# A two-layer graph network on one core: layer 2 gathers raw rows first, normalisation is stored behind it, and the table work is spread differently

## The chip, the cores and the metric

One of the eight cores of a Trainium2 chip runs the kernel. The metric is the device time of one execution in microseconds (us), less being better. The profile is of one such execution. TensorE appears in it as PE (weight loads as PEld), VectorE as DVE, ScalarE as ACT, GpSimd as POOL; SP issues most of the DMAs, in order, ACT and POOL issue some.

## The reference, cut to what matters

There are N = 6250 nodes with 128 features and E = 106250 edges, sorted by target node. Two attention layers ("conv") run over the edges, with a normalisation over all nodes between them:

```python
rel_t_enc = jnp.cos((last_update[src] - t)[:, None] * time_w[None, :] + time_b)
edge_attr = jnp.concatenate([rel_t_enc, msg], axis=-1)          # 32 + 64 columns
h = _transformer_conv(x, edge_attr, src, dst, Wq1, ..., bs1)     # 2 heads
mu = h.mean(axis=0)
var = ((h - mu) ** 2).mean(axis=0)
h = (h - mu) / jnp.sqrt(var + 1e-05) * bn_g + bn_b               # per feature, over all nodes
h = jax.nn.relu(h)
return _transformer_conv(h, edge_attr, src, dst, Wq2, ..., bs2)
# around it: layernorm(x + that), row by row
# _transformer_conv: q = h Wq + bq, k = h Wk + bk, v = h Wv + bv, e = edge_attr We, all in 2 heads;
#   alpha = q[dst] . (k[src] + e) / 8; softmax over the edges of a target;
#   out = segment_sum(a * (v[src] + e)) + h Ws + bs
```

Layer 2 can't begin with normalised rows before the last node of layer 1 is done, because the mean and the variance are over all nodes.

## The kernel before

**Chunks and rounds.** The edges are cut into 107 chunks (NC) of 1024 edges, each with at most 64 target nodes. `conv(c, extra)` runs a software pipeline of rounds k = -4 to 109, written out by hand: each engine executes its instructions in the order in which the rounds emit them. In round k chunk k+4 is fetched and gathered, chunk k+1 is transposed, chunk k is scored, chunk k-1 is summed and chunk k-2 is finished.

- `fetch(k)` (L720 to L738): SP issues the DMAs of the edge attributes into `ff`, of the table rows into `ftab`, and in layer 2 of the stored time encoding `fz`, of the transposed attributes (into `fxT`) and of the residual rows `fr`. `ff` and `ftab` have six buffers.
- `gather(k)` (L743): eight indirect DMAs of 128 source rows each, issued by POOL; from `xv_d` in layer 1, from `h_d` in layer 2.
- `turn_in` (L792, L798): TensorE transposes the gathered rows and, in layer 1, the attributes; ACT copies them out of PSUM (L793, L799). The PSUM tiles of these, of the turned weights (L832) and of the extra work come from one pool of four banks.
- `score`, `lowest`, `weigh` (L809, L810, L815, L817, L822): the scores, their row minimum `flow` on DVE, and the exponential on ACT.
- `gather_sums` (L839), `divide` (L844 to L847, giving `fa`), `finish_turn` (L853, L854, and the copy `fat`, L856), `finish` (L863 on): the weighted sums. In layer 1, `finish` adds the residual table into `fres` (L869) and stores 64 columns of `hT` by a DMA (L870).

**The time encoding** exists in layer 1 alone. `encode(j)` is nine DVE instructions (L760 to L768); `sine()` is one ACT instruction (L774) that writes `fzs`, after a load of the sine's table (ACT_TABLE_LOAD; the exponential loads its own again). In the next round `place()` copies `fzs` into `ff` (DVE, L779) and stores it to `enc_d` (SP, L780). Up to chunk 26 (SINGLE = 24, and three more) one chunk is encoded per sine and per round; after that two chunks share a sine, every second round. `fzs` has two buffers.

**Tables and other extra work.** Layer c's queries are folded with the key weights into table rows per node, in 13 blocks of 512 nodes (`tables`): four or five matmuls (L627), each followed by an ACT instruction (L631, L629) or a DVE one (L633) into `fo`, then a store to `tab_d` (L637, issued by ACT). They are yielded step by step by `rest()` and pulled by the rounds, `pull(extra, 1)` per round, six steps more at the first round of layer 1. Layer 2's blocks have five steps, the last a residual (`residual`, L1030 to L1033). Blocks 0 and 1 of layer 2 are made before its pipeline begins, through a single PSUM bank.

**Between the layers** come, in this order: a sum of `hT` (half on DVE, half on ACT, L983), the squares (L988), the square root and four small steps, then 13 blocks of scaling with Relu on ACT (L1003), transposing (L1006), copying to `fhr` (L1008, four buffers) and storing to `h_d` (L1011, L1014). Layer 2's first gather waits for all of `h_d`.

Of the kernel before, what the change touches and what calls it, by code (L numbers as in the profile page):

```python
# [7 lines left out]
F32 = mybir.dt.float32  # L8
# [612 lines left out]

def tables(nc, pl, c, fT, b0, work, bank):

    o = work.tile([P, GE, H, 3 - c], F32, name="fo", tag="fo")
    for i, (a, b) in enumerate(pl.mats[c]):
        pg = bank()
        nc.tensor.matmul(pg, a, fT, start=True, stop=True)  # L627
        if i == 2 * H:
            nc.scalar.activation(o[:, :, :, 2], pg[:, :, None].to_broadcast([P, GE, H]), AF.Identity, bias=b)  # L629
        elif i < H:  # L630
            nc.scalar.activation(o[:, :, i, 0], pg, AF.Identity, bias=b)  # L631
        else:
            nc.vector.scalar_tensor_tensor(  # L633
                o[:, :, i - H, 1].rearrange("p (b n) -> p b n", n=P), pg.rearrange("p (b n) -> p b n", n=P), b,
                pl.code[:, None, :].to_broadcast([P, GE // P, P]), op0=OP.add, op1=OP.add)
        if i == len(pl.mats[c]) - 1:
            nc.scalar.dma_start(pl.tab_d[c][:, b0 * GE:(b0 + 1) * GE], o)  # L637
        yield
# [22 lines left out]
def ordered(ctx: ExitStack, tc: tile.TileContext, pl, x, dst, edge_attr_64, conv2, bn_g, bn_b, out):  # L661
# [9 lines left out]
    const = ctx.enter_context(tc.tile_pool(name="fconst", bufs=1))  # L671
    dram = ctx.enter_context(tc.tile_pool(name="fdram", bufs=1, space=bass.MemoryType.DRAM))
    h_d = dram.tile([N, D], F32, name="h_d")
    res_d = dram.tile([NP, D], F32, name="res_d")

    enc_d = dram.tile([NC, P, T * TD], F32, name="enc_d")
# [14 lines left out]

    SINGLE = 24

    def conv(c, extra):


        cs = ExitStack()
# [42 lines left out]
        def gather(k):  # L740
            f = ch[k].f
            for t in range(T):
                nc.gpsimd.indirect_dma_start(  # L743
                    out=f[:, t, (1 if c else 0):1 + D], out_offset=None, in_=h_d if c else pl.xv_d,
                    in_offset=bass.IndirectOffsetOnAxis(ap=pl.srcs[:, t, k:k + 1], axis=0))

        shape = [P, T, TD]
# [22 lines left out]
        def sine():  # L770
            arg, *of = args
            args.clear()
            z = work.tile([P, 2, T, TD], F32, name="fzs")
            nc.scalar.activation(z[:, :len(of)], arg[:, :len(of)], AF.Sin, bias=qpi)  # L774
            turned.extend((k, z[:, i]) for i, k in enumerate(of))

# [6 lines left out]
        def turn_in(k, u):  # L783

            s = ch[k]
            if u == 0:
                s.ft = work.tile([P, CE], F32, name="fft")
                if c == 0:
                    s.et = work.tile([EC, CE], F32, name="fet")
            px = p_tr.tile([P, GE], F32, name="fpx", tag="tr")  # L790
            for t in range(4):
                nc.tensor.transpose(px[:, t * P:(t + 1) * P], s.f[:, u * 4 + t, 1:1 + D], ident)  # L792
            nc.scalar.copy(s.ft[:, u * GE:(u + 1) * GE], px)  # L793
            if c:
                return
            pe = p_tr.tile([P, GE], F32, name="fpe", tag="tr")
            for t in range(4):
                nc.tensor.transpose(pe[:EC, t * P:(t + 1) * P], s.f[:, u * 4 + t, 1 + D:], ident)  # L798
            nc.scalar.copy(s.et[:, u * GE:(u + 1) * GE], pe[:EC])  # L799
            if u:  # L800
                nc.sync.dma_start(et_d[k], s.et)
# [39 lines left out]
        def divide(k):  # L841
            s = ch[k]
            inv = small.tile([P, 1], F32, name="finv")
            nc.vector.tensor_scalar(inv, s.pa[:, D + ED:], 1e-30, None, op0=OP.max)  # L844
            nc.vector.reciprocal(inv, inv)
            s.a = small.tile([P, D + EW], F32, name="fa")
            nc.vector.tensor_scalar(s.a, s.pa, inv, None, op0=OP.mult)  # L847

        def finish_turn(k):
            s = ch[k]  # L850
# [60 lines left out]
        with cs, tc.manual_schedule():  # L911
            for k in range(-AHEAD, NC + 3):
# [3 lines left out]
                if on(k + AHEAD):  # L916
                    fetch(k + AHEAD)
                    gather(k + AHEAD)
                if k == -AHEAD and c == 0:
                    pull(extra, 6)  # L920
                if on(k):
                    score(k, 0)
                if on(k - 1):
# [16 lines left out]
                for j in (k + 2,) if k < SINGLE else (k + 2, k + 3) if k == SINGLE else (k + 3,):  # L940
                    if c == 0 and on(j):
                        encode(j)
                        if j < SINGLE + 3:
                            sine()
                pull(extra, 1)
                if len(args) == 3 or args and k == NC - 4:
                    sine()
                if on(k - 2):
                    finish(k - 2)
                if c and on(k):  # L950
                    nc.vector.tensor_copy(ch[k].f[:, :, 1 + D:1 + D + TD], ch[k].z)
                for _ in range(min(len(done), 2 if k > NC - 12 else 1)):
                    store(*done.pop(0))
                if on(k - 1):
                    gather_sums(k - 1)
            for _ in extra:
                pass
            for rows in done:
# [5 lines left out]
    with tc.tile_pool(name="fpw", bufs=2) as pw:  # L964
        with tc.tile_pool(name="ftp", bufs=3, space=bass.MemoryType.PSUM) as mp, tc.manual_schedule():
            turn_features(nc, pl, mp, N)
        def rest():
            for b0 in range(1, NT):
                yield from tables(nc, pl, 0, xT[:, b0 * GE:(b0 + 1) * GE], b0, pw, lambda: pl.bank())
                if b0 == 2:  # L970
                    yield from load_others(nc, pl, const, conv2, bn_g, bn_b)
            yield from matrices(nc, pl, 1, const, lambda: pl.bank()[:, :P])

        conv(0, rest())
    nc.gpsimd.memset(hT[:, N:], 0.0)


    with tc.tile_pool(name="fbn1", bufs=1) as one, tc.tile_pool(name="fbnw", bufs=2) as pw:
        neg = one.tile([P, 2], F32, name="fmu")
        half = N // 2  # L980
        scr = pl.xT
        nc.vector.tensor_reduce(neg[:, 0:1], hT[:, :half], AX.X, OP.add)
        nc.scalar.activation(scr[:, half:N], hT[:, half:N], AF.Copy, accum_out=neg[:, 1:])  # L983
        mu = one.tile([P, 1], F32, name="fmu1")
        nc.vector.tensor_add(mu, neg[:, 0:1], neg[:, 1:])
        nc.vector.tensor_scalar(mu, mu, -1.0 / N, None, op0=OP.mult)
        var = one.tile([P, 1], F32, name="fbvar")
        nc.scalar.activation(scr[:, :N], hT[:, :N], AF.Square, bias=mu, accum_out=var)  # L988
        nc.vector.tensor_scalar(var, var, 1.0 / N, EPS, op0=OP.mult, op1=OP.add)
        nc.scalar.activation(var, var, AF.Sqrt)  # L990
        scale = one.tile([P, 1], F32, name="fscale")
        nc.vector.reciprocal(scale, var)
        nc.vector.tensor_mul(scale, scale, pl.bng)
        shift = one.tile([P, 1], F32, name="fshift")
        nc.vector.tensor_mul(shift, scale, mu)
        nc.vector.tensor_add(shift, shift, pl.bnb)
        NB = -(-N // P)
        with tc.tile_pool(name="fbnh", bufs=4) as hp, \
                tc.tile_pool(name="fbnp", bufs=2, space=bass.MemoryType.PSUM) as pps:
            for b0 in range(0, NB, 4):  # L1000
                n = min(4, NB - b0)
                cs_ = slice(b0 * P, b0 * P + GE)
                nc.scalar.activation(hT[:, cs_], hT[:, cs_], AF.Relu, bias=shift, scale=scale)  # L1003
                pt = pps.tile([P, 4, P], F32, name="fpt")
                for i in range(n):
                    nc.tensor.transpose(pt[:, i], hT[:, (b0 + i) * P:(b0 + i + 1) * P], ident)  # L1006
                hr = hp.tile([P, 4, P], F32, name="fhr")
                nc.vector.tensor_copy(hr[:, :n], pt[:, :n])  # L1008
                full = min(n, (N - b0 * P) // P)
                if full:  # L1010
                    nc.sync.dma_start(h_d[b0 * P:(b0 + full) * P, :].rearrange("(b p) d -> p b d", p=P), hr[:, :full])  # L1011
                if full < n:
                    left = N - (b0 + full) * P
                    nc.sync.dma_start(h_d[(b0 + full) * P:N, :], hr[:left, full])  # L1014

        def residual(b0):

# [21 lines left out]
            next(res, None)  # L1039
            yield  # L1040

        with tc.tile_pool(name="fpp2", bufs=1, space=bass.MemoryType.PSUM) as pp:
            pl.bank = lambda: pp.tile([P, GE], F32, name="fpg")
            for b0 in range(2):
                for _ in block(b0):
                    pass

        def rest():
            for b0 in range(2, NT):
                yield from block(b0)  # L1050

        conv(1, rest())
    nc.sync.dma_start(out[N - NN:N, :], tail_d[NN:2 * NN, :])


@with_exitstack
def tile_gnn_resnorm(ctx: ExitStack, tc: tile.TileContext, x, src, dst, edge_attr_64, edge_weight, node_vec,
# [13 lines left out]
    with tc.tile_pool(name="plan", bufs=1) as pl, tc.tile_pool(name="planw", bufs=2) as mw, \  # L1071
# [5 lines left out]
                                                  ap=[[step, r1 - r0], [1, P]]))  # L1077
        NP = got.NP = -(-(N + NN) // GE) * GE
        got.hT = keep.tile([P, NP], F32, name="fhT")
        got.rest = keep.tile([P, 1 + D], F32, name="fxrest")  # L1080
        got.raw, got.web, got.ws, got.mats = {}, {}, {}, ([], [])

# [22 lines left out]
        nc.vector.tensor_scalar(ident, jpp, 0.0, None, op0=OP.is_equal)  # L1105
        nxt = pl.tile([P, NC], F32, name="nxt")
        nc.vector.tensor_scalar(nxt, jpp[:, :NC], 1.0, None, op0=OP.is_equal)
        ones = pl.tile([P, P], F32, name="pones")
        nc.vector.memset(ones, 1.0)
        ends = pl.tile([1, 2, NC + 1], F32, name="ends")  # L1110
        nc.vector.memset(ends[:, 0, NC:], float(N))
# [154 lines left out]
```

## Time and profile before

| | us |
|---|---|
| median of 11 runs (2327.93 to 2334.68) | 2332.75 |
| the profiled execution, its own time | 2332.44 |
| its span | 2330.3 |
| first and last gather issued, layer 1 | 38.2, 1145.5 |
| first and last gather issued, layer 2 | 1220.5, 2290.4 |
| row minimum L815 of chunk 2, 26 and 106, layer 1 | 90.05, 349.60, 1175.46 |
| busy: PE, POOL, DVE, ACT | 2226.6, 1639.5, 1224.5, 1222.1 |

2.1 us of the time lie outside the span. A round can be read as the distance between two row minima L815, since each chunk has one. A matmul's end is modelled, so that a full PE row says that PE had work queued, not that it was at its peak.

### The profile page before, as it was taken

Reading aid. Unit: us, or ns where it says so; the run is one execution under the profiler, and the core shown is the slowest. Engines: PE = TensorE matmul, PEld = TensorE weight load, DVE = VectorE, ACT = ScalarE, POOL = GpSimd, SP = SyncE. Lnnn points to the kernel's source line nnn. Section 1 sums busy time; section 2 is a strip of 40 time slices with the busy share of each in tenths; the row PEclk is TensorE's granted clock in tenths of the full one; section 3 lists DMA queues with packets and bytes.
Section 4 is the critical chain, followed back from the end, with each engine's and each line's share of the span. In section 5 each row is a group of like instructions: output and inputs, shape, how many; then the busy total and the mean of one; then the engine's idle time right before and its main releaser. Section 6 shows DMA issues by size and latency. Waiting matters only on the chain.

```text
span 2330.3 us, 39250 instructions
## 1 busy us (share of the span) xinstructions
PE 2226.6 (96%) x11637; PEld 1715.4 (74%) x11637; DVE 1224.5 (53%) x3735; ACT 1222.1 (52%) x1950; POOL 1639.5 (70%) x1733
## 2 busy tenths in 40 slices
PE   6899999999999999999958999999999999999997
PEld 4778878788787888878844777777777777776765
DVE  5667677677676766666633443433343333333333
ACT  3667776666655555555543444444444444343444
POOL 3777777777777777777507777777777777777772
PEclk8999999999999999999977999999999999999999
DMA  8666666666665665665529667776667666656561
GB/s 256 173 154 185 178 191 189 181 180 179 180 181 159 163 160 156 166 160 157 141 71 247 176 186 194 191 189 189 183 180 188 166 164 165 166 155 161 156 155 36
DMA packets 428354, 396.58 MB, mean 170 GB/s; under 512 B 282064, under 2 KB 371940, under 8 KB 424804
## 3 DMA queue, kind: packets, MB, share of 16 engines
q1 hardware_dynamic: 354406, 238.66, 37.0%
q0 software_dynamic: 55168, 114.12, 20.4%
q10 hardware_dynamic: 18558, 41.20, 5.0%
q8 instruction: 95, 1.56, 0.3%
q14 instruction: 127, 1.04, 0.1%
HBM read 279.72 MB, written 110.59 MB: 167 GB/s over the span
## 4 chain that ended last, share of the span: by engine, by line
PE 40%; POOL 4%; DMA 4%; issue 2%; DVE 1%; ACT 1%; POOLq 0%; ACTq 0%; DVEq 0%
PE fpa L839 13%; PE fps L809 7%; PE fps L810 7%; POOL ff L743 4%; PE fpx L792 3%; PE fppt L832 3%; DMA ff<-h_d,fsrcs 3%; PE fpg L627 2%; PE fpo L875 2%; PE fpo L876 1%; PE fpg L1030 1%; PE fpo L853 0%; PE fpo L854 0%; DVE flow L815 0%; DMA h_d<-fhr 0%
## 5 line engine op out<-in xcount | busy, mean ns | idle before, releaser
L743 POOL DMA_INDIRECT ff<-xv_d,fsrcs x856 | 824.7, 963 | 311.0 <-issue 212.8
L743 POOL DMA_INDIRECT ff<-h_d,fsrcs x856 | 810.2, 946 | 290.5 <-issue 258.8
L839 PE MATMUL fpa<-ff,fpt 128*128 128x225 f32 x3424 | 700.0, 357 | 0.0
L839 PEld LDWEIGHTS fpa<-ff,fpt 128*128 128x128 f32 x3424 | 633.4, 190 | 11.1 <-issue 0.5
L833 ACT COPY fpt<-fppt 128x512 f32<-128x512 f32 x428 | 229.4, 588 | 464.8 <-PE fppt L832 463.5
L809 PE MATMUL fps<-fft,ftab 128*128 128x512 f32 x856 | 445.2, 602 | 5.2 <-ACT fs L822 5.2
L793 ACT COPY fft<-fpx 128x512 f32<-128x512 f32 x428 | 249.0, 582 | 378.8 <-PE fpx L792 375.4
L856 DVE COPY fat<-fpo 128x256 f32<-128x256 f32 x214 | 90.9, 425 | 577.9 <-PE fpo L854 573.9
L822 ACT ACTIVATE fs<-fps,fm 128x1024 f32<-128x1024 f32 x214 | 238.6, 1115 | 88.0 <-DVE fm L817 87.0
L832 PEld LDWEIGHTS fppt<-fident,fs 128*128 128x128 f32 x1712 | 200.1, 140 | 105.9 <-issue 105.6
L815 DVE TENSOR_REDUCE flow<-fps 128x1 f32<-128x1024 f32 x214 | 260.1, 1215 | 9.8 <-PE fps L810 9.8
L792 PE MATMUL fpx<-fident,ff 128*128 128x128 f32 x1712 | 246.6, 274 | 15.0 <-DMA ff<-h_d,fsrcs 14.5
L832 PE MATMUL fppt<-fident,fs 128*128 128x128 f32 x1712 | 222.2, 272 | 0.0
L810 PE MATMUL fps<-fet,ftab 112*128 112x512 f32 x428 | 219.2, 593 | 0.0
L810 PE MATMUL fps<-fxT,ftab 112*128 112x512 f32 x428 | 219.1, 593 | 0.0
L792 PEld LDWEIGHTS fpx<-fident,ff 128*128 128x128 f32 x1712 | 198.6, 141 | 24.8 <-DMA ff<-h_d,fsrcs 20.8
L809 PEld LDWEIGHTS fps<-fft,ftab 128*128 128x128 f32 x856 | 167.7, 225 | 8.0 <-ACT fs L822 6.0
L810 PEld LDWEIGHTS fps<-fet,ftab 112*128 112x128 f32 x428 | 107.3, 251 | 76.0 <-issue 59.8
L810 PEld LDWEIGHTS fps<-fxT,ftab 112*128 112x128 f32 x428 | 84.3, 197 | 99.7 <-issue 99.5
L767 DVE SCALAR_TENSOR_TENSOR farg<-fturns,farg 128x256 f32<-128x256 f32 x321 | 136.6, 426 | 11.0
L844 DVE TENSOR_SCALAR finv<-fpa 128x1 f32<-128x1 f32 x214 | 32.8, 153 | 206.3 <-issue 94.9
L798 PE MATMUL fpe<-fident,ff 128*112 128x128 f32 x856 | 130.7, 276 | 7.7 <-DVE ff L779 5.1
(198 smaller groups left out, 2272.3 us busy)
## 6 DMA issues: line engine op xcount, KB each, us to landing
ff<-in_edge_attr SPq DMA_DIRECT2D x214, 256.0 KB
et_d<-fet SPq DMA_DIRECT2D x107, 448.0 KB
fxT<-et_d SPq DMA_DIRECT2D x107, 448.0 KB
ftab<-tab_d SPq DMA_DIRECT2D x107, 192.0 KB
tab_d<-fo ACTq DMA_DIRECT2D x13, 1536.0 KB
ff<-xv_d,fsrcs POOLq DMA_INDIRECT x856
enc_d<-fzs SPq DMA_DIRECT2D x107, 128.0 KB
ff<-h_d,fsrcs POOLq DMA_INDIRECT x856
```

Source lines behind the costliest of these rows:

```text
L743: nc.gpsimd.indirect_dma_start(out=f[:, t, (1 if c else 0):1 + D], out_offset=None, in_=h_d if c else pl.xv_d, in_offset=bass.IndirectOffs ...
L767: nc.vector.scalar_tensor_tensor(arg, turn, -part, arg, op0=OP.mult, op1=OP.add)
L792: nc.tensor.transpose(px[:, t * P:(t + 1) * P], s.f[:, u * 4 + t, 1:1 + D], ident)
L793: nc.scalar.copy(s.ft[:, u * GE:(u + 1) * GE], px)
L798: nc.tensor.transpose(pe[:EC, t * P:(t + 1) * P], s.f[:, u * 4 + t, 1 + D:], ident)
L809: nc.tensor.matmul(s.ps[:, w], s.tab[:, :, 0], s.ft[:, w], start=True, stop=False)
L810: nc.tensor.matmul(s.ps[:, w], s.tab[:EC, :, 1], s.et[:, w], start=False, stop=True)
L815: nc.vector.tensor_reduce(low, s.ps, AX.X, OP.min)
L822: nc.scalar.activation(s.s, s.ps, AF.Exp, bias=s.bias, scale=-1.0)
L832: nc.tensor.transpose(pp[:, t * P:(t + 1) * P], s.s[:, at:at + P], ident)
L833: nc.scalar.copy(s.pt[:, u * GE:(u + 1) * GE], pp)
L839: nc.tensor.matmul(s.pa, s.pt[:, t * P:(t + 1) * P], s.f[:, t, 1:1 + D + EW], start=t == 0, stop=t == T - 1)
```

## The change

Layer 1's rounds now also transpose finished blocks of `hT`, take their moments (`bn_stats`) and store them raw to `h_d`. The first three chunks of layer 2 gather from `h_d` and are normalised after the gather: by ACT on the way out of PSUM, and in place on DVE (`normalise`, three instructions on 128x1024). Meanwhile all rows are normalised, transposed and stored to `hn_d`, from which the other chunks gather. The sums and squares over the whole of `hT` are replaced by one `bn_aggr` over the blocks' moments, and scale and shift are spread over partitions by two DVE steps, two matmuls and a copy. `turned_rows` makes four transposes and one DVE copy of a block, `put_rows` its DMA. One block of tables instead of two stands ahead of layer 2, with three PSUM banks; no step is pulled before round 0, then two per round up to round 3 and after round 80, and each block is followed by two empty steps. `fo` and `fzs` have one buffer, and the row tile `fhr` is in a pool of two.

```diff
 def tables(nc, pl, c, fT, b0, work, bank):
-    o = work.tile([P, GE, H, 3 - c], F32, name="fo", tag="fo")
+    o = work.tile([P, GE, H, 3 - c], F32, name="fo", tag="fo", bufs=1)
...
+    RAW = 3
-    def conv(c, extra):
+    def conv(c, extra, first_blocks=None):
...
-                    out=f[:, t, (1 if c else 0):1 + D], out_offset=None, in_=h_d if c else pl.xv_d,
+                    out=f[:, t, (1 if c else 0):1 + D], out_offset=None, in_=(h_d if k < RAW else hn_d) if c else pl.xv_d,
...
-            z = work.tile([P, 2, T, TD], F32, name="fzs")
+            z = work.tile([P, 2, T, TD], F32, name="fzs", bufs=1)
...
-            nc.scalar.copy(s.ft[:, u * GE:(u + 1) * GE], px)
+            if c and k < RAW:
+                nc.scalar.activation(s.ft[:, u * GE:(u + 1) * GE], px, AF.Relu, bias=pl.shift, scale=pl.scale)
+            else:
+                nc.scalar.copy(s.ft[:, u * GE:(u + 1) * GE], px)
...
+        def normalise(k):
+            rows = ch[k].f[:, :, 1:1 + D]
+            for i, op in enumerate((OP.mult, OP.add)):
+                nc.vector.tensor_tensor(rows, rows, pl.spread[:, None, i].to_broadcast([P, T, D]), op)
+            nc.vector.tensor_scalar(rows, rows, 0.0, None, op0=OP.max)
...
-                if k == -AHEAD and c == 0:
-                    pull(extra, 6)
+                if k == -AHEAD and c:
+                    first_blocks()
...
-                pull(extra, 1)
+                if k >= 0:
+                    at_round[0] = k
+                    pull(extra, 2 if k < 4 or k > 80 else 1)
...
                 if c and on(k):
+                    if k < RAW:
+                        normalise(k)
...
+        def pass_rows(b0):
+            r0 = b0 * GE
+            n = min(GE, N - r0)
+            rows = turned_rows(b0)
+            nc.vector.bn_stats(stats[:, b0], hT[:, r0:r0 + n])
+            yield
+            put_rows(h_d, b0, rows)
+            yield
...
         def rest():
+            others = load_others(nc, pl, const, conv2, bn_g, bn_b)
             for b0 in range(1, NT):
                 yield from tables(nc, pl, 0, xT[:, b0 * GE:(b0 + 1) * GE], b0, pw, lambda: pl.bank())
-                if b0 == 2:
-                    yield from load_others(nc, pl, const, conv2, bn_g, bn_b)
+                for _ in range(2):
+                    next(others, None)
+                    yield
             yield from matrices(nc, pl, 1, const, lambda: pl.bank()[:, :P])
+            for b0 in range(-(-N // GE)):
+                while at_round[0] < 3 + max(k for k in range(NC) if first(k)[0] < (b0 + 1) * GE):
+                    yield
+                yield from pass_rows(b0)
         conv(0, rest())
...
...
+        moments = const.tile([P, 2], F32, name="fmom")
+        nc.vector.bn_aggr(moments, stats)
...
+        def relu(b0):
+            r = slice(b0 * GE, (b0 + 1) * GE)
+            nc.scalar.activation(hT[:, r], hT[:, r], AF.Relu, bias=shift, scale=scale)
+        def first_blocks():
+            for b0 in range(1, NT):
+                relu(b0)
+            for b0 in range(-(-N // GE)):
+                put_rows(hn_d, b0, turned_rows(b0))
-        with tc.tile_pool(name="fpp2", bufs=1, space=bass.MemoryType.PSUM) as pp:
-            for b0 in range(2):
-                for _ in block(b0):
-                    pass
+        with tc.tile_pool(name="fpp2", bufs=3, space=bass.MemoryType.PSUM) as pp, tc.manual_schedule():
+            relu(0)
+            for _ in block(0):
+                pass
...
         def rest():
-            for b0 in range(2, NT):
+            for b0 in range(1, NT):
                 yield from block(b0)
+                yield
+                yield
-        conv(1, rest())
+        conv(1, rest(), first_blocks)
```

More of the change, by code (lines that the diff above doesn't have):

```diff
@@ L673, in ordered @@
     h_d = dram.tile([N, D], F32, name="h_d")
+    hn_d = dram.tile([N, D], F32, name="hn_d")
+    at_round = [0]
+    stats = const.tile([P, -(-N // GE), 6], F32, name="fstats")
     res_d = dram.tile([NP, D], F32, name="res_d")
@@ L955, in conv @@
                     gather_sums(k - 1)
+            at_round[0] = 2 * NC
             for _ in extra:
@@ L966, in ordered, with turned_rows @@
             turn_features(nc, pl, mp, N)
+        def pass_rows(b0):
[6 more added lines that the diff above has]
+            yield
+        def turned_rows(b0):
+            r0 = b0 * GE
+            n = -(-min(GE, N - r0) // P)
+            pt = pl.bank().rearrange("p (b d) -> p b d", d=P)
+            for i in range(n):
+                nc.tensor.transpose(pt[:, i], hT[:, r0 + i * P:r0 + (i + 1) * P], ident)
+            rows = pw.tile([P, GE // P, P], F32, name="fhr")
+            nc.vector.tensor_copy(rows[:, :n], pt[:, :n])
+            return rows
@@ L967, in rest, with put_rows @@
+        def put_rows(to, b0, rows):
+            r0 = b0 * GE
+            n = min(GE, N - r0)
+            full = n // P
+            if full:
+                nc.sync.dma_start(to[r0:r0 + full * P, :].rearrange("(b p) d -> p b d", p=P), rows[:, :full])
+            if n > full * P:
+                nc.sync.dma_start(to[r0 + full * P:N, :], rows[:n - full * P, full])
         def rest():
+            others = load_others(nc, pl, const, conv2, bn_g, bn_b)
             for b0 in range(1, NT):
                 yield from tables(nc, pl, 0, xT[:, b0 * GE:(b0 + 1) * GE], b0, pw, lambda: pl.bank())
-                if b0 == 2:
-                    yield from load_others(nc, pl, const, conv2, bn_g, bn_b)
+                for _ in range(2):
+                    next(others, None)
+                    yield
@@ L972, in rest @@
             yield from matrices(nc, pl, 1, const, lambda: pl.bank()[:, :P])
+            for b0 in range(-(-N // GE)):
+                while at_round[0] < 3 + max(k for k in range(NC) if first(k)[0] < (b0 + 1) * GE):
+                    yield
+                yield from pass_rows(b0)
         conv(0, rest())
[L975 to L992, printed above, removed]
-        nc.vector.tensor_mul(scale, scale, pl.bng)
[L994 to L1014, printed above, removed]
@@ new lines, in ordered @@
+        moments = const.tile([P, 2], F32, name="fmom")
+        nc.vector.bn_aggr(moments, stats)
+        std = const.tile([P, 1], F32, name="fstd")
+        nc.vector.tensor_scalar(std, moments[:, 1:], EPS, None, op0=OP.add)
+        nc.scalar.activation(std, std, AF.Sqrt)
+        scale = pl.scale = const.tile([P, 1], F32, name="fscale")
+        nc.vector.reciprocal(scale, std)
+        nc.vector.tensor_mul(scale, scale, pl.bng)
+        shift = pl.shift = const.tile([P, 1], F32, name="fshift")
@@ L1016, in residual @@
+        nc.vector.tensor_mul(shift, scale, moments[:, 0:1])
+        nc.vector.tensor_sub(shift, pl.bnb, shift)
         def residual(b0):
@@ L1040, in block @@
             yield
-        with tc.tile_pool(name="fpp2", bufs=1, space=bass.MemoryType.PSUM) as pp:
-            pl.bank = lambda: pp.tile([P, GE], F32, name="fpg")
-            for b0 in range(2):
-                for _ in block(b0):
-                    pass
+        def relu(b0):
[7 more added lines that the diff above has]
+        with tc.tile_pool(name="fpp2", bufs=3, space=bass.MemoryType.PSUM) as pp, tc.manual_schedule():
+            pl.bank = lambda: pp.tile([P, GE], F32, name="fpg")
+            relu(0)
+            for _ in block(0):
+                pass
+            diag = const.tile([P, 2, P], F32, name="fdiag")
+            spread = pl.spread = const.tile([P, 2, P], F32, name="fspread")
+            pb = pp.tile([P, 2, P], F32, name="fpb", bufs=1)
+            for i, col in enumerate((scale, shift)):
+                nc.vector.tensor_scalar(diag[:, i], ident, col, None, op0=OP.mult)
+                nc.tensor.matmul(pb[:, i], pl.ones, diag[:, i], start=True, stop=True)
+            nc.vector.tensor_copy(spread, pb)
         def rest():
-            for b0 in range(2, NT):
+            for b0 in range(1, NT):
                 yield from block(b0)
-        conv(1, rest())
+                yield
+                yield
+        conv(1, rest(), first_blocks)
     nc.sync.dma_start(out[N - NN:N, :], tail_d[NN:2 * NN, :])
@@ L1079, in tile_gnn_resnorm @@
         got.hT = keep.tile([P, NP], F32, name="fhT")
+        nc.gpsimd.memset(got.hT[:, N:], 0.0)
         got.rest = keep.tile([P, 1 + D], F32, name="fxrest")
@@ L1107, in tile_gnn_resnorm @@
         nc.vector.tensor_scalar(nxt, jpp[:, :NC], 1.0, None, op0=OP.is_equal)
-        ones = pl.tile([P, P], F32, name="pones")
+        ones = got.ones = keep.tile([P, P], F32, name="pones")
         nc.vector.memset(ones, 1.0)
```

## The prediction

> **What bounds the kernel now.** I read the page's slices first, then the two layers' gathers, then one round of layer 1 and the border between the layers in the timeline.
>
> ```profile
> PE   6899999999999999999958999999999999999997
> POOL 3777777777777777777507777777777777777772
> PEclk8999999999999999999977999999999999999999
> ```
>
> PE is full but for the start and one hole in the middle; only there does its clock drop. The hole is the border between the layers.
>
> ```profile
> L743 POOL DMA_INDIRECT ff<-xv_d,fsrcs x856: 938/944/1194, 38.2 to 1145.5; - x172
> L743 POOL DMA_INDIRECT ff<-h_d,fsrcs x856: 940/944/1399, 1220.5 to 2290.4; - x172
> ```
>
> These rows answer for the gathers' tile. Layer 2's 856 gathers take 1070 us, 1.25 us each, 10.0 per chunk of eight: POOL never waits there. Its row minima L815 stand 10.14 us apart while table steps run and 9.28 after them, so PE first falls behind and then catches POOL up: layer 2 ends when its gathers end, wherever they began. Layer 1 differs: 107 chunks at 10.0 would be 1070 us, and its gathers take 1107. There PE sets the pace: rounds of 9.83 us without a table step, 10.69 with one (0.86 us of PE each). Here is one such round of the first 27, in which each round has its own sine:
>
> ```profile
> 197.23 1.22 DVE L815 TENSOR_REDUCE flow<-fps 128x1 f32<-128x1024 f32 x1
> 201.81 1.28 ACT L774 ACT_TABLE_LOAD   x1
> 202.39 0.54 DVE L869 TENSOR_TENSOR fres<-fpo,ftab 64x64 f32<-64x64 f32 x2
> 202.95 0.34 SPq L731 DMA_DIRECT2D ftab<-tab_d  x1
> 203.10 0.51 ACT L774 ACTIVATE fzs<-farg,qpi 128x256 f32<-128x256 f32 x1
> 203.41 0.36 SPq L780 DMA_DIRECT2D enc_d<-fzs  x1
> 203.64 0.29 DVE L779 COPY ff<-fzs 128x256 f32<-128x256 f32 x1
> 204.36 0.45 DVE L847 TENSOR_SCALAR fa<-fpa,finv 128x225 f32<-128x225 f32 x1
> 207.16 0.27 PE L853 MATMUL fpo<-fident,fa 128*128 128x128 f32 x1
> 207.92 1.21 DVE L815 TENSOR_REDUCE flow<-fps 128x1 f32<-128x1024 f32 x1
> ```
>
> The reader should see the order in SP's queue. The store of `fzs` (L780) stands behind the table fetch (L731), which waits for `fres` (ends 202.93). So the store at 203.41 is not that of the sine at 203.10 but of the sine one round earlier: counting both from the start, store 13 leaves at 203.41 and sine 14 starts at 203.10. With two buffers that harms nobody, and DVE's `fa` is ready 2.35 us before PE asks for it at 207.16.
>
> Last, the border:
>
> ```profile
> 1190.27 2.81 ACT L983 ACTIVATE fxT<-fhT 128x3125 f32<-128x3125 f32 x1 [9.32 <-DMA fhT<-fres]
> 1201.63 9.28 ACT L1003 ACTIVATE fhT<-fhT,fshift,fscale 128x512 f32<-128x512 f32 x13 [0.87 <-DVE fshift L996]
> 1220.55 0.95 POOL L743 DMA_INDIRECT ff<-h_d,fsrcs  x1 [29.91 <-issue]
> 1228.16 0.36 ACTq L637 DMA_DIRECT2D tab_d<-fo  x1
> 1250.52 0.94 POOL L743 DMA_INDIRECT ff<-h_d,fsrcs  x1 [0.30 <-issue]
> ```
>
> Layer 1's last `hT` store lands at 1190.2; the first gather starts 30.4 us later, chunk 3's first (1250.52) 60.3 us later.
>
> **The border, changed: -18.7 us.** Let L be the landing of the last `hT` store. Raw rows of the earlier blocks are stored by then; the last block needs one transpose, one copy, one small DMA (3.4 us from issue to use, from L1014 at 1215.85 to SP's next step at 1219.2) and POOL's start 1.3 us after that, so chunk 0's gather starts near L+6 and POOL has chunks 0 to 2 out at L+36. Chunk 3 needs all of `hn_d`. Its chain: transpose, copy, `bn_stats`, `bn_aggr` (no row shows either; by the DVE rows of 128x106, 0.24, and 128x512, 0.69, they cost 0.2 to 0.7 each; I take 0.3, the small form being nearer), square root and five small steps of 0.2: L+2.6. ACT then has eight scalings of 0.71 (9.28/13), two L631 of 1.16 and an issue of 0.4 before the table store: L+11.8. SP's table fetch of chunk 0 waits for its landing (1228.16 to 1232.26: 4.1), and with three more issues behind it the first `hn_d` store leaves at L+17.9. All 14 stores stand in SP's queue there, ahead of chunk 1's fetch. `fhr` now has two buffers: copy 0.69 plus store 2.5 to 2.7 (issue 1206.33, its buffer's next copy 1208.82) make 3.4 us per two blocks; six such turns, a small last store of 2.3 and POOL's start give L+41.6. So chunk 3 comes 60.3 - 41.6 = 18.7 earlier. Bounds: a gain of 24 if the stores keep up and only the 30 us of gathers count; 9 if each store takes the 4.1 us that one took before. PE's own start is earlier too (its first transposes stand behind the 13 blocks, at about L+32, against 1251.07, L+60.9), chunk 1's fetch leaves at L+39 against L+46.8, and the three `normalise` steps (by L815's 1.22 for 1024 elements, 3.7 us per chunk) lie on a DVE that is under 40% busy there; without that cover they would cost 11. Relu instead of a copy out of PSUM is 0.71 against 0.58, six times, on an idle ACT.
>
> **Layer 2: 0.** Five table steps in seven rounds give PE 9.28 + 0.86 x 5/7 = 9.9 per round, under POOL's 10.0. POOL sets the pace and the end moves with its start.
>
> **`fzs` with one buffer: +52.** Sine n must now wait for store n-1, and the sine's table load with it, since in the changed program's instruction order the wait stands on the load. In rounds 2 to 25, where the table fetch is held by `fres`, a turn closes: row minimum to end of `fres` 5.70 (197.23 to 202.93); to the store's issue 0.48; the store's packets end 2.1 to 2.9 after issue in these rounds, median 2.35, and I take 2.45 with its signal; load 1.28 and sine 0.51, with 0.1 between; then from the sine's end to the next row minimum 2.14, which one round shows where the sine came last:
>
> ```profile
> 128.77 0.51 ACT L774 ACTIVATE fzs<-farg,qpi 128x256 f32<-128x256 f32 x1
> 130.62 0.30 PE L853 MATMUL fpo<-fident,fa 128*128 128x128 f32 x1 [1.84 <-DVE fa L847]
> 131.41 1.21 DVE L815 TENSOR_REDUCE flow<-fps 128x1 f32<-128x1024 f32 x1
> ```
>
> Together 12.6 us per round, against PE's 9.83 or 10.69. What is queued behind the waiting load on ACT: the sine, a table step, the two copies of turned weights (PE's sums and PSUM banks wait for them); behind the sine on DVE: L779, `divide`, and so PE's L853. The 24 rounds from minimum 2 to 26 took 349.60 - 90.05 = 259.6. Now 24 x 12.6 = 302.4, six rounds with a DVE table step before `fres` at 0.97 more (the store leaves 7.15 instead of 6.18 after the minimum), and one round that encodes twice, 3.3: 311.5. After round 26 two chunks share a sine every second round, so that about ten microseconds lie between store and sine, and nothing waits. The cheap end for this cost is zero (then these rounds take 254, the pace of PE alone); the dear end is 13.4 per round, with stores of 2.9 and half-clocked matmuls on the way: +71.
>
> At this place a page speaks. In the rows, the load takes 1.28 us and the sine starts 0.01 after it. The Trainium skill, "ScalarE: Activation LUTs", section "What ACT_TABLE_LOAD costs", adds a drain of some 1.38 us to each switch. By it, as an estimate, the 24 rounds would cost another 33 us; I go by the rows.
>
> **The rest of layer 1: +11.6, and 0.75 at its end.** Rounds 0 to 2: four table steps now fall into rounds 0 and 1, where two ACT ones (1.16 each) stand before the copies for PE's first sums, and 0.86 of PE each: +2.9. Rounds 26 to 106 took 1175.46 - 349.60 = 825.9, some 7 of it late waits for gathers. Now: 80 x 9.83 = 786.4; the 38 table steps left at 0.86, 32.7; layer 2's matrices as before, 5; eleven blocks of `pass_rows` at four transposes (0.12 each), 5.5; and 5 for their 1.3 us on DVE (copy 0.69, `bn_stats` 0.6) in rounds where a sine stands just before: 834.6, +8.7. PE is ahead of nothing it could make up: POOL needs 10.15 per chunk there. Block 11's copy and moments delay the last `fres` by 0.75. Hidden, all at nothing: SP's 14 raw stores (0.36 each, in a queue with room), the earlier memset (0.44 on an idle POOL), and `fo` with one buffer, whose store (5.6 to 7.7 us) has a whole round before the next write.
>
> **The sum** against the profiled execution: 2332.44 + 2.9 + 52.0 + 8.7 + 0.75 - 18.7 = 2378.1. That execution lies 0.3 us under the median; I say 2378. About 0.2% (5 us) is what a measurement of this kernel can tell from no change.
>
> **Rivals.**
> 1. *The sine's wait does not bind* (its store gets out before the table fetch, or lands in time). Then -5.5 takes the place of +52: 2320.6, faster. For it: with two buffers the trace has no such wait. Against it: store 13 after sine 14. It turns on one number: the turn has to fall below 10.6 us, which the store would reach only by leaving 2 us earlier than the end of `fres` lets it.
> 2. *The clock falls as well.* In the round above, 1.84 us of idle PE was followed by 3.4 us at half clock (131.06 to 134.47), with four L792 in 0.87 instead of 0.60. Now each such round idles 2 to 3 us. One slow stretch costs PE some 1.7 and still fits (9.83 + 0.86 + 1.7 = 12.4); two per round make 14.1, 36 more: 2414. By the Trainium skill, "TensorE: Matmul & The Clock Gate", Part 1, the clock falls after an idle window of 3.4 us; by that estimate it would not fall here at all, while the row shows it after 1.84.
> 3. *The border gives nothing back* (`hn_d` late, or chunk 3 held by a later DMA): 2397.
>
> **How the numbers follow.** Forecast 0.76; rival 1 0.11; rival 2 0.06; rival 3 0.07. The forecast's own range is 2356 to 2398 (turn of 11.9 to 13.4, border 9 to 24). Rival 3 lies inside it; rivals 1 and 2 are left out: 2350 to 2399. Faster 0.11, same 0.02, slower 0.87.
>
> **What would show it.** Right: row minima of layer 1's chunks 3 to 26 about 12.6 apart, ACT's idle time before the sine's table load ended by the `enc_d` store, PE at 8 tenths in slices 3 to 7, the last `hT` landing near 1255, chunk 3's gather 42 us after it, layer 2 at 10.0 per chunk. Wrong: minima at 10.4 there, or a first gather of `hn_d` 60 us after the landing.

## The result, and the profile after

The changed kernel takes 2386.07 us (median of 8 runs, 2384.05 to 2388.25), the kernel before in the same session 2332.3: a ratio of 1.0232 (95% interval 1.0223 to 1.0241), slower by 54 us. The forecast was 2378, in a range of 2350 to 2399. The profiled execution has a span of 2384.9 us, 54.6 more than before.

The page's slices first:

```profile
PE   5888888999999999999996999999999999999996
POOL 3766555777777777677724777777777777777772
PEclk7999999999999999999997999999999999999998
```

PE is at 8 tenths in the third to seventh slice, where it was at 9: in them lie most of the rounds in which each chunk has a sine of its own. The hole in the middle is still there and narrower. The gathers' rows, from the view of their line, now L748 (duration least/median/most, first and last start):

```profile
L748 POOL DMA_INDIRECT ff<-xv_d,fsrcs x856: 938/944/1197, 39.0 to 1212.0; - x172
L748 POOL DMA_INDIRECT ff<-h_d,fsrcs x24: 940/944/1007, 1264.3 to 1293.1; - x24
L748 POOL DMA_INDIRECT ff<-hn_d,fsrcs x832: 940/944/1482, 1302.7 to 2344.4; - x167
```

Layer 1's last gather is issued 66.5 us later than before (1212.0 against 1145.5), layer 2's last one 54.0 later: the border gave some of it back, and between chunk 3's first gather and the last one lie 1041.7 us against 1039.9. Now one of layer 1's early rounds, from the timeline (start, duration, idle time before it and what ended it):

```profile
340.97 1.22 DVE L823 TENSOR_REDUCE flow<-fps 128x1 f32<-128x1024 f32 x1
345.98 0.54 DVE L883 TENSOR_TENSOR fres<-fpo,ftab 64x64 f32<-64x64 f32 x2
346.55 0.34 SPq L736 DMA_DIRECT2D ftab<-tab_d  x1
346.94 0.43 SPq L785 DMA_DIRECT2D enc_d<-fzs  x1
349.53 1.28 ACT L779 ACT_TABLE_LOAD   x1 [4.00 <-DMA enc_d<-fzs]
350.82 0.51 ACT L779 ACTIVATE fzs<-farg,qpi 128x256 f32<-128x256 f32 x1
352.18 0.45 DVE L855 TENSOR_SCALAR fa<-fpa,finv 128x225 f32<-128x225 f32 x1
352.78 0.30 PE L867 MATMUL fpo<-fident,fa 128*128 128x128 f32 x1 [1.72 <-DVE fa L855]
353.57 1.21 DVE L823 TENSOR_REDUCE flow<-fps 128x1 f32<-128x1024 f32 x1
```

The round is 12.60 us long. Read it from row minimum to row minimum as a closed turn: 5.55 to the end of `fres`, 0.42 to the store's issue behind the table fetch, 2.59 until ACT's table load may start, 1.80 to the end of the sine, 2.24 to the next minimum. Before, the load (then L774) stood ahead of the store in time. Now ACT is idle for 4.00 us in front of it, and then PE waits for `fa`. The view of waits for these rounds (window 91 to 409 us; in total, times, longest) says the same in sum:

```profile
ACT L779 <- DMA enc_d<-fzs: 104.5, 24, 8.0
DVE ff L784 <- ACT fzs L779: 99.6, 24, 4.8
```

Last, the border:

```profile
1258.29 0.49 SPq L884 DMA_DIRECT2D fhT<-fres  x1
1260.09 0.47 PE L1002 MATMUL fpg<-fident,fhT 128*128 128x128 f32 x1 [2.84 <-DMA fhT<-fres]
1264.30 0.94 POOL L748 DMA_INDIRECT ff<-h_d,fsrcs  x1 [51.39 <-ACT fhT L1074]
1277.87 20.33 SPq L1012 DMA_DIRECT2D hn_d<-fhr  x12
1282.68 0.69 DVE L1004 COPY fhr<-fpg 128x512 f32<-128x512 f32 x1 [6.31 <-DMA hn_d<-fhr]
1299.19 0.26 SPq L1014 DMA_DIRECT2D hn_d<-fhr  x1
1302.70 0.94 POOL L748 DMA_INDIRECT ff<-hn_d,fsrcs  x1 [8.69 <-issue]
```

The last `hT` store lands at about 1260. The first raw gather starts 4 us after that, the first store to `hn_d` leaves 17.9 after it, the copies for these stores wait for their two buffers (L1004), and chunk 3's first gather starts 42.7 after it, where it was 60.3. Before it POOL stands still for 8.69 us.

Four of the experiments (e9 to e12) had first run in an hour when the kernel before itself took 2854 us, with engines standing in all rounds for no cause that the trace shows; those four runs (ratios 0.9861, 0.9883, 0.9997 and 0.9852) carry no conclusion here, and the same kernels were run again.

### The profile page after: what moved, and what is told of

Same layout as the page of the kernel before. It is cut to its first block, busy times and chain, and to the rows that moved or that the text cites. A ratio compares the mean times of both kernels' runs of the same rounds, so it can differ in the third digit from the quotient of the medians.

```text
span 2384.9 us, 39406 instructions
## 1 busy us (share of the span) xinstructions
PE 2249.6 (94%) x11690; PEld 1735.2 (73%) x11690; DVE 1250.3 (52%) x3771; ACT 1210.6 (51%) x1946; POOL 1640.3 (69%) x1733
## 3 DMA queue, kind: packets, MB, share of 16 engines
q0 software_dynamic: 55168, 114.12, 19.8%
## 5 line engine op out<-in xcount | busy, mean ns | idle before, releaser
L748 POOL DMA_INDIRECT ff<-xv_d,fsrcs x856 | 823.1, 962 | 378.4 <-issue 217.3
L748 POOL DMA_INDIRECT ff<-hn_d,fsrcs x832 | 789.3, 949 | 262.0 <-issue 229.1
L797 PE MATMUL fpx<-fident,ff 128*128 128x128 f32 x1712 | 255.0, 280 | 17.6 <-DMA ff<-hn_d,fsrcs 10.0
L797 PEld LDWEIGHTS fpx<-fident,ff 128*128 128x128 f32 x1712 | 203.8, 144 | 29.8 <-DMA ff<-hn_d,fsrcs 17.9
```

The source lines that it names most:

```text
L748: nc.gpsimd.indirect_dma_start(out=f[:, t, (1 if c else 0):1 + D], out_offset=None, in_=(h_d if k < RAW else hn_d) if c else pl.xv_d, in_o ...
```

## The experiments

**Theory A**, the forecast's: each sine, and its table load, waits for the store of the sine before, which stands in SP's queue behind a table fetch that `fres` holds up. **Rivals**: B, the work that the change adds to layer 1 is what costs; C, the lower clock in these rounds (0.95 granted between 91 and 409 us) is a cause. For the border the theory is that the end of layer 2 moves with the time from which POOL can gather without a hole.

**e1_sine_two.** Undo one word of the change.

```diff
-            z = work.tile([P, 2, T, TD], F32, name="fzs", bufs=1)
+            z = work.tile([P, 2, T, TD], F32, name="fzs")
```

> The changed kernel with two buffers for the sine's result instead of one, nothing else. Theory A (the sine and its table load wait for the store of the sine before): the 24 rounds from row minimum 2 to 26, 317.8 us in the changed kernel, fall to PE's own pace of 9.83 to 10.69 each, some 256, so about 62 us less: 2324 us, between 2318 and 2332, a little faster than before; ACT's idle time in front of the sine's table load ended by the store disappears. Rival B (the work that the change adds to layer 1, the moved table steps, transposes and moments, is what costs): over 2360, rounds 3 to 26 still above 12. Rival C (the lower granted clock there is the cause and not a result): the clock in these rounds stays near 0.95 and the time near 2375.

Measured: 2319.76 us, a ratio of 0.9958 (0.9944 to 0.9971) to before. Minimum 2 to minimum 26 take 253.5 us, where the changed kernel takes 317.8. A round of it:

```profile
188.55 0.55 DVE L883 TENSOR_TENSOR fres<-fpo,ftab 64x64 f32<-64x64 f32 x2
188.70 1.28 ACT L779 ACT_TABLE_LOAD   x1 [0.67 <-issue]
189.12 0.35 SPq L736 DMA_DIRECT2D ftab<-tab_d  x1
189.51 0.43 SPq L785 DMA_DIRECT2D enc_d<-fzs  x1
```

The load starts 0.81 us ahead of the store of the sine before. Theory A holds. B falls: the added work is all still there, and the change without the one-buffer sine is faster than before by 11.5 us. C falls: with the wait gone the granted clock between 91 and 409 us is 1.00, so the lower clock came with the wait.

**e2_before_sine_one.** The same word alone, in the kernel before.

```diff
-            z = work.tile([P, 2, T, TD], F32, name="fzs")
+            z = work.tile([P, 2, T, TD], F32, name="fzs", bufs=1)
```

> The kernel before with one buffer for the sine's result instead of two, nothing else. Theory A: rounds 3 to 26 take 12.6 to 13.2 us as in the changed kernel, +52 to +58: 2384 to 2391. Rival B (it takes the rest of the change as well, for instance its other order of table steps, to make the wait bind): within 10 us of 2332. Rival C: as B, with a clock of 0.99 in these rounds.

Measured: 2394.6 us, a ratio of 1.0269 (1.0255 to 1.0283), more than the whole change costs and a little above the 2384 to 2391 expected. The 24 rounds take 318.6 us against 259.6, as in the changed kernel. The view of waits, same columns as above, window 91 to 400 us:

```profile
ACT L774 <- DMA enc_d<-fzs: 103.5, 23, 8.0
```

Between the two profiled executions, 65 us apart, 59 lie in those rounds. Most of the rest, 3.4 in rounds 26 to 106 and 3.4 behind the first gather of layer 2, is not explained.

**e3_store_at_sine.** One buffer, but the store takes another place in SP's queue.

```diff
             nc.scalar.activation(z[:, :len(of)], arg[:, :len(of)], AF.Sin, bias=qpi)
             turned.extend((k, z[:, i]) for i, k in enumerate(of))
+            for i, k in enumerate(of):
+                nc.sync.dma_start(enc_d[k].rearrange("p (t d) -> p t d", d=TD), z[:, i])
...
         def place():
             for k, z in turned:
                 nc.vector.tensor_copy(ch[k].f[:, :, 1 + D:1 + D + TD], z)
-                nc.sync.dma_start(enc_d[k].rearrange("p (t d) -> p t d", d=TD), z)
```

> The changed kernel, still with one buffer, but the store of the sine's result to enc_d is issued right behind the sine, ahead of the next round's table fetch in SP's queue, instead of behind it. Theory A1 (the place in SP's queue makes the turn: the store waits for fres through the table fetch ahead of it): the store leaves some 8 us before the next sine, the wait is gone, 2318 to 2335. Rival A2 (one buffer costs by itself, through the store's 2.4 us and its signal or the copies that read the buffer): rounds 3 to 26 stay above 12, over 2365.

Measured: 2319.38 us, 0.9953 (0.9939 to 0.9966), the same as with two buffers. Its timeline:

```profile
190.03 0.51 ACT L779 ACTIVATE fzs<-farg,qpi 128x256 f32<-128x256 f32 x1
190.57 0.34 SPq L782 DMA_DIRECT2D enc_d<-fzs  x1
199.93 1.28 ACT L779 ACT_TABLE_LOAD   x1 [1.08 <-issue]
```

The store leaves 0.03 us after its sine, 9.4 ahead of the next table load. So a single buffer is no cost by itself; the place of the store in the queue made it one.

**e11_single8.** One buffer and the store where the changed kernel has it, but sines in pairs from an earlier round on.

```diff
-    SINGLE = 24
+    SINGLE = 8
```

> The changed kernel, still with one buffer for the sine's result and the store in its place, but chunks share a sine in pairs from round 9 on and no longer only from round 25. Theory A (the wait binds only where each round has its own sine, so that the sine follows the store by 2.6 us; with one sine in two rounds there are about ten us between them): rounds 3 to 8 stay at 12.6 to 14, rounds 10 to 24 return to 9.83 or 10.69; 16 rounds times 2.7 less, 2343, between 2335 and 2350. Rival F (any sine on one buffer waits for the store): over 2370. Rival G (chunks encoded one round earlier wait for their gathers while POOL is still behind): some of the 43 us is given back, as waits of DVE for ff's gathers, 2350 to 2370.

Measured: 2343.05 us, 1.0054 (1.0037 to 1.0070). The rounds from minimum 2 to 8 take 12.6 to 13.8 us, the one that encodes twice 16.8, the one behind it 13.2, and from then on they take 9.83 or 10.69: minimum 2 to 26 in 277.7 us instead of 317.8. The wait needs a sine in every round; F and G fall.

**e4_two_and_raw4.** As e1, and one more raw chunk.

```diff
-    RAW = 3
+    RAW = 4
```

> As the first kernel of this call (two buffers for the sine's result), and four chunks of layer 2 gather raw rows instead of three. In the changed kernel POOL stands still for 8.4 us between the last raw gather (issued until 1294.3) and chunk 3's first gather (1302.7), which waits for the last hn_d store. Theory A (layer 2 ends when its gathers end): with a fourth raw chunk POOL runs through, chunk 4's first gather comes 40 us after chunk 0's, and the time is 8 us under the first kernel of this call: 2316. Rival D (PE, which waits behind the 13 blocks of transposes, or the fourth normalise step on DVE sets the pace of layer 2's start): equal to the first kernel within 3 us. Rival E (without a hole POOL's gathers and the hn_d stores slow each other): slower than the first kernel.

(The "first kernel" of this expectation is e1_sine_two.) Measured: 2313.08 us, 0.9924 (0.9911 to 0.9938), 6.7 under e1. POOL goes from raw to normalised rows without a hole, chunk 4 following chunk 3:

```profile
1237.63 0.94 POOL L748 DMA_INDIRECT ff<-h_d,fsrcs  x1 [0.30 <-issue]
1238.88 0.95 POOL L748 DMA_INDIRECT ff<-hn_d,fsrcs  x1 [0.30 <-issue]
```

Chunk 3's first gather comes 30.0 us after chunk 0's, in e1 37.4. Of these 7.4 us 2.2 are lost again later: from there to the last gather it takes 1044.3 us, in e1 1042.1.

**e10_raw1.** As e1, but with `RAW = 1`: the border's gain made smaller.

> As e1_sine_two (the changed kernel with two buffers for the sine's result, 0.9958 of the kernel before), but only chunk 0 of layer 2 gathers raw rows; chunks 1 and 2 wait for the last hn_d store with all later ones. Theory A (the end of layer 2 moves with the time from which POOL can gather without a hole): chunk 1 starts where chunk 3 did, 37.4 us after chunk 0, so chunk 3 comes 20 us later than in e1_sine_two and so does the end: 2340, 8 to 9 us over the kernel before, for layer 1's added work. Rival D (PE, not POOL, paces the first chunks, or the two normalise steps saved on DVE give it back): within 8 us of 2320.

Measured: 2337.47 us, 1.0028 (1.0019 to 1.0038). Chunk 3's first gather comes 57.1 us after chunk 0's, 19.8 later than in e1, and the time is 17.7 longer. Theory A: POOL's start sets the end of layer 2; D would have had 2328 at most.

**e12_rows_three.** As e1, with one more buffer for the turned rows.

```diff
-            rows = pw.tile([P, GE // P, P], F32, name="fhr")
+            rows = pw.tile([P, GE // P, P], F32, name="fhr", bufs=3)
```

> As e1_sine_two (0.9958 of the kernel before, three raw chunks), with three buffers instead of two for the turned rows that are stored to h_d and hn_d. Theory J (the 14 stores of the normalised rows go at the pace of two buffers, 3.4 us per two blocks): three blocks per turn of 3.4 us, chunk 3's first gather 31 to 33 us after chunk 0's instead of 37.4, so 4 to 6 us less: 2315. Rival K (PE's transposes at half clock, 1.1 us a block, with their PSUM buffers, or the stores' own bytes set the pace): chunk 3 at 36 to 37 us, 2318 to 2320.

Measured: 2315.0 us, 0.9931 (0.9918 to 0.9944). The first 12 stores to `hn_d` are through in 15.71 us instead of 20.4, and chunk 3's first gather comes 33.0 after chunk 0's, not 37.4:

```profile
1213.51 15.71 SPq L1012 DMA_DIRECT2D hn_d<-fhr  x12
1229.72 0.26 SPq L1014 DMA_DIRECT2D hn_d<-fhr  x1
1234.36 0.94 POOL L748 DMA_INDIRECT ff<-hn_d,fsrcs  x1 [3.31 <-issue]
```

Theory J: two buffers set the pace of the stores. With three, POOL's hole is 3.31 us.

**e9_pull_later.** As e4, with one step of extra work per round until round 85. The changed kernel shows why, in rounds 82 and 83, which take 16.94 and 14.28 us; two rows of the first:

```profile
996.75 0.79 PE L595 MATMUL fpg<-ftr,ftr 64*128 64x128 f32 x2 [2.28 <-ACT fft L801]
999.29 5.24 PE L847 MATMUL fpa<-ff,fpt 128*128 128x225 f32 x16
```

The second step of the round takes its PSUM bank from the pool that the copies `fft` empty, and waits 2.28 us for one; then sixteen matmuls take 5.24 us, where they take 3.21 in an undisturbed round. The wait and the slow matmuls are two things, as e10 shows, where the same instructions run in these rounds. There the wait is as long, but the granted clock stays at 1.00 (in the changed kernel it is 0.50 from 996.6 to 1003.4), and the two rounds take 14.25 and 12.61 us:

```profile
932.17 0.48 PE L595 MATMUL fpg<-ftr,ftr 64*128 64x128 f32 x2 [2.28 <-ACT fft L801]
934.06 3.21 PE L847 MATMUL fpa<-ff,fpt 128*128 128x225 f32 x16
```

```diff
-                    pull(extra, 2 if k < 4 or k > 80 else 1)
+                    pull(extra, 2 if k < 4 or k > 85 else 1)
```

> As e4_two_and_raw4 (two buffers for the sine's result, four raw chunks; 2313.1 us), but two steps of the extra work per round are pulled only from round 86 on instead of 81, so that layer 2's matrices take one step per round. In e4_two_and_raw4 the rounds 82 and 83 take 16.9 and 14.3 us: PE waits 2.3 us for a PSUM buffer between the two steps, and runs at half clock after it. Theory H (that wait and the clock after it make those rounds long): they return to 10 to 11 us, 8 to 10 us less, 2304. Rival I (POOL's gathers or the store of hT set the pace there, or the last transposes come too late for layer 1's end): 2310 to 2316.

Measured: 2313.46 us, 0.9911 (0.9898 to 0.9925), some 3 us under e4 by the ratios, whose intervals overlap. The time lies in rival I's range and not at H's 2304. The trace shows more than the times: rounds 82 to 85 take 9.9 to 10.6 us, but the last step for the matrices falls into round 86, where two are pulled again, and the wait is back for that one round of 14.98:

```profile
972.60 0.66 PE L1002 MATMUL fpg<-fident,fhT 128*128 128x128 f32 x4 [2.28 <-ACT fft L801]
973.63 4.80 PE L847 MATMUL fpa<-ff,fpt 128*128 128x225 f32 x16
```

So the wait of H is shown: it goes where one step is pulled and comes back where two are. What it is worth is not: minimum 78 to 92 take 147.5 us against 153.0 in e4, but e1 and e10, with the double steps, take 150.4 and 148.7; there the clock fell for less time or not at all. The ratio is the lowest of all runs, but its interval overlaps those of e4 and e12.

## Why the prediction was right, point by point

The terms of the sum, against the two profiled executions:

| stretch | forecast | measured |
|---|---|---|
| start to minimum 2 | +2.9 | +1.0 (91.03 against 90.05) |
| minimum 2 to 26 | +52 | +58.3 (317.8 against 259.6) |
| minimum 26 to 106 | +8.7 | +10.2 (836.1 against 825.9) |
| minimum 106 to chunk 3's first gather | +0.75 - 18.7 | -17.3 (57.7 against 75.1) |
| from there to the last gather, and to the end | 0 | +1.8 and +0.6 |
| sum | +45.6 | +54.6 |

**The sine's wait.** The mechanism is shown by e1, e2 and e3 from three sides, and rival 1's time of 2320.6, for a wait that does not bind, is what e1 has: 2319.8. Too small was the turn. Its parts, as medians over rounds 3 to 24, are 5.69, 0.42, 2.63, 1.80 and 2.14 us; the forecast had 5.70, 0.48, 2.45, 1.89 and 2.14. The mean round is longer, 13.26: 6.05 to the end of `fres` and 2.73 from the store's issue to the load. This last is the mis-sized term. I had put the store's end at 2.35 after its issue and 0.1 for its signal; 2.73 instead of 2.45 makes 6.7 us in 24 rounds, as much as the whole miss of this term (6.3). The other parts nearly cancel, among them 1.4 us of the sum's own: the five parts add up to 12.66 per round, and it went on with 12.6. The Trainium skill, "DMA: Bandwidth & Descriptors", section "Anatomy of one DMA — SWDGE (gpsimd) path", gives 2.0 us fixed and the bytes at 436 GB/s for a DMA issued from GpSimd; by it, as an estimate, 128 KB take 2.3 us, and these stores from SP took 2.63 in the median and 2.73 in the mean, from issue to the start of ACT's load.

**The table load's drain.** From the load's start to the sine's end it takes 1.80 us in every one of these rounds, 1.28 and 0.51 and nothing between. The page's further 1.38 us, weighed in the prediction, shows in none of them.

**The border.** The forecast had the first `hn_d` store at L+17.9 and chunk 3 at L+41.6, measured 17.9 and 42.7. The first was met with some luck: the steps listed up to the table store add up to L+11.0, not to the 11.8 written, and it left at L+11.7 because nine scalings, not eight, stand ahead of it. What follows is as forecast: the 3.4 us per two blocks that made most of this is shown by e12, the ends that it sets by e4 and e10. `normalise` costs 3.2 us per chunk (two of 1.24, one of 0.69), not 3.7, and is hidden as forecast.

**The rest of layer 1.** The sum was near by luck, its parts were not: I took 5 us for layer 2's matrices "as before", but two of their steps per round after round 80 make a wait for a PSUM bank and slow matmuls after it, and rounds 80 to 83 are 11.9 longer than at 9.83 (7.5 in e10, where the clock did not fall). The blocks of raw rows cost less than forecast, 0.44 us in each of their rounds instead of 1, and the two errors nearly cancel.

**Rival 2, the clock.** The granted clock between minimum 2 and 26 was 0.95, before 0.99: it stood at 0.50 in seven stretches of 3.4 or 6.8 us and not in every round, and the 36 us that two slow stretches per round would have added did not come. **Rival 3** is out: the border gave 17. The range was stated too narrow at its dear end: a turn of 13.4 together with a border of 9 makes 2407, not 2398.

## What to carry to other kernels

When a tile goes from two buffers to one, ask who empties it, in which queue that reader stands and what is ahead of it there: here a store of 0.4 us of issue stood behind a fetch that waited for the end of another chunk, and that turned one saved buffer into 60 us. Issuing the store where its data arise cost nothing here (e3) and made the one buffer as good as two. At a border between stages, find the engine that sets the pace behind it, and count only from when that engine can run without a hole: here each microsecond of POOL's earlier start was nearly a microsecond of the kernel.

## What the runs showed of the hardware

After 2.28 us of idle PE, sixteen 128x225 matmuls took 5.24 and 4.80 us instead of 3.21, the granted clock being 0.50 for 6.8 and 3.4 us (changed kernel, e9); after the same wait in e10 it stayed at 1.00 and they took 3.21. The Trainium skill, "TensorE: Matmul & The Clock Gate", Part 1, has the clock fall after an idle window of about 3.4 us; here matmuls were slow after less.

What tells the cases apart is where the wait lies: in all ten profiles told of here the granted clock changes on a grid of 3.41 us. Leaving out the first and last 60 us of each, every such window at full clock in which PE was busy for at most 0.41 of the time was followed by half clock (58 windows), none above 0.66 was, and between 0.42 and 0.66 both occur. The wait of 2.28 us lies within one window in e9 and, but for 0.16 us, in the changed kernel (0.33 and 0.38 busy); in e10 it lies across two (0.54 and 0.63). So it was the busy share of a window, not the length of one wait, that went with the fall; PE's busy time is modelled, which may blur the bound.

The kernel before has no rows of these: `bn_stats` over 128x512 takes 0.68 us, over 128x106 0.27, and `bn_aggr` over thirteen blocks 0.51.
